# Laying the blank rows of a mixture-of-experts buffer after 12 of 16 token tiles, 640 rows for each expert

## The chip, the core and the metric

The kernel runs on one core of a Trainium2 chip. A core has five engines with instruction queues of their own: TensorE (PE, matrix products; its weight loads are listed apart as PEld), VectorE (DVE), ScalarE (ACT), GpSimd (POOL) and SyncE (SP), which here only issues transfers. Transfers run on 16 DMA engines. Engines wait for one another, and for transfers, through semaphores. Times are device microseconds for the whole program. The profiler's record of one execution gives its span, what each engine did when, and what it waited for.

## The reference

The input `x` has 8 sequences of 256 tokens with 128 numbers each, 2048 tokens in all. Two layers follow, each with a cross-attention to `ctx_1024` and a mixture of experts:

```
x = x + attention0(layernorm(x), ctx)     # 16 heads of 8, a hash mask
x = x + experts0(layernorm(x))            # 8 experts, 512 hidden, relu, biases
x = x + attention1(layernorm(x), ctx)     # 16 heads of 64, causal
x = x + experts1(layernorm(x))            # 8 experts, 352 hidden, silu gate
```

In both expert parts a linear router gives each token 8 logits. The two largest pick its two experts, and their softmax gives the two weights. The layer's output is the weighted sum of the two experts' outputs. So each layer has 4096 (token, expert) pairs.

## The kernel before

**The buffers.** The tokens are 16 tiles of 128 (`NT`). For every layer there is a DRAM tensor `xs` that holds one row of 130 numbers for each pair: the normalised token, the row of `ys` to which its result belongs, and its weight. Each expert has a region of 2176 rows (`XT`) in it, filled from the start. Experts work on tiles of 128 rows, and the last tile of each region is filled only in part. The rest of that tile must hold rows that do no harm: zeros, with a spare row of `ys` as the place of the result. These are the blank rows. A template of 128 of them per expert lies in the DRAM tensor `blank`.

**Routing.** `route` (line 552) handles two or four token tiles: layer norm with both copies of each row written to an SBUF tile `rows` (line 394), the logits, the two maxima, ranks from a matrix product with a triangle, and the running counts `taken`, which hold the number of rows of each expert before every tile. GpSimd then scatters the rows to `xs` (line 644, one indirect DMA for each tile and choice). `norm_T` leaves `lead` steps between the variance and the normalised rows, since GpSimd computes the power in between (line 383).

**Placing.** `place(l, True)` (line 651) runs once 12 tiles (`NEARLY`) are routed. It makes a table of expert tiles that are already full; 16 in layer 0 and 17 in layer 1 (`EARLY`) are worked on from this early table. `place(l, False)` makes the table of the rest (of 39) once all 16 tiles are routed. `tails(l)` (line 696) follows it: it turns the final counts into integers (`last`, line 699), and for each expert loads the count into a register and copies its 128 blank rows behind the last used row (line 706). Four of these copies are issued by SP and four by ACT.

**Experts.** For each expert tile, SP loads its expert and row from the table (line 719), fetches the rows (`xj`, line 733) and the expert's first weights (`wj`, line 740); TensorE flips `xj` (line 745), makes the hidden layer (line 760 in layer 0, 770 and 773 in layer 1) and the result (line 793); VectorE weighs it (line 798), and GpSimd scatters it to `ys` (line 800). Fetches run four tiles ahead of use. `fetch` of the first late tile first lets the side steps run until `tails` has been written down.

**Order.** Every engine runs its instructions in the order in which the program writes them; that order is made by hand. Main loops write the large steps, and `side` is a list of generators of which `tick` runs one step each. `one_by_one` chains generators so that one starts when the one before has ended. In attention 1 a unit (four heads' worth of scores on 256 queries) writes its score products (line 902), four minima on VectorE (`least`, line 917), exponentials on ACT (line 928), and in later units the normalisation on GpSimd (line 941), the flips (line 951) and the values (line 966). Two `tick`s stand in each unit.

**Dependencies.** Waits between transfers that touch the same DRAM tensor follow from the order of writing, unless the kernel declares them disjoint. `free` declares a write disjoint from the others of its key, `after` makes a read wait for the listed writes. A row at an offset held in a register counts as touching the whole tensor.

Of the kernel before, what the change touches and what calls it, by code (L numbers as in the profile page):

```python
# [17 lines left out]
P = 128  # L18
B = 8
S = 256  # L20
QT = S // P
# [11 lines left out]
NT = T // P  # L33
NJ = (2 * T + E * (P - 1)) // P
ROW = D + 2
XT = T + P
NX = E * XT + E * P
# [4 lines left out]
NEARLY = NT - 4  # L42
EARLY = (16, 17)
# [19 lines left out]
def kernel(  # L63
# [28 lines left out]
    nc = tc.nc  # L92
# [20 lines left out]
    known = {}  # L113
# [11 lines left out]
            )  # L125
        return dma

    def free(key, dma, by_index=True):

        tc.declare_no_dep(dma.ins, group=key, reason="disjoint rows")  # L130
        tc.add_to_no_dep_group(key, dma.ins)
        if by_index:
            tc.declare_no_dep(dma.ins, group=key + "read", reason="disjoint rows")
            if key in known:
                tc.add_to_no_dep_group(key + "late", dma.ins)
        writes.setdefault(key, []).append(dma)


    side = []

    def tick():
        for g in list(side):
            if next(g, side) is side:
                side.remove(g)
# [8 lines left out]
    def one_by_one(g):  # L153


        def run():
            while turn:
                yield from turn[0]
                turn.pop(0)

        turn.append(g)
        if len(turn) == 1:
            side.append(run())

    def drain():
        while side:
# [9 lines left out]
    xt = [xb[i // QT][:, i % QT, :] for i in range(NT)]  # L176
# [194 lines left out]
    def norm_T(tiles, name, rows=None, lead=2):  # L371
        n = len(tiles)
        mv = sm.tile([P, GT, 2], F32, tag="mv", name=f"mv{name}", bufs=3)
        for i, t in enumerate(tiles):
            st = sm.tile([P, 6], F32, tag="bn", name=f"st{name}_{i}", bufs=3)
            nc.vector.bn_stats(out=st, in_=t)
            nc.vector.bn_aggr(out=mv[:, i, :], in_=st)
            if i == 1 and n > 2:
                yield
        ve = sm.tile([P, GT], F32, tag="ve", name=f"ve{name}", bufs=3)  # L380
        nc.vector.tensor_scalar(ve[:, :n], mv[:, :n, 1], EPS, None, ALU.add)
        rs = sm.tile([P, GT], F32, tag="rs", name=f"rs{name}", bufs=3)
        nc.gpsimd.tensor_tensor(rs[:, :n], ve[:, :n], mhalf[:, :n], ALU.pow)
        for _ in range(lead):
            yield
        xns = []
        for i, t in enumerate(tiles):
            if rows is None:
                xn = sm.tile([P, D], F32, tag="xn", name=f"xn{name}_{i}", bufs=4)
                to = xn  # L390
            else:
                xn = rows[:, i, 0, :D]
                to, t = rows[:, i, :, :D], t.unsqueeze(1).to_broadcast([P, 2, D])
            nc.vector.tensor_scalar(to, t, mv[:, i, 0:1], rs[:, i : i + 1], ALU.subtract, ALU.mult)
            xns.append(xn)
            if i == 1 and n > 2:
                yield
        for _ in range(1 if rows is None else 2):
            yield
        pt = bank("pt", f"np{name}")  # L400
        for i, xn in enumerate(xns):
            nc.tensor.transpose(pt[:, ts(i, P)], xn, ident)
        tag, bufs = (f"xnT{n}", 2) if rows is None else (f"xnTr{n}" if n == QT else f"xnT{n}", 1)
        xnT = wk.tile([P, n * P], F32, tag=tag, name=f"xnT{name}", bufs=bufs)
        nc.scalar.copy(xnT, pt[:, : n * P])
        yield
        return xnT
# [144 lines left out]
    def route(l, t0, GT, eng=nc.vector):  # L552

        name = f"{l}_{t0}"
# [1 line left out]
        tiles = slice(t0, t0 + GT)  # L556
        rows = wk.tile([P, G // P, 2, ROW], F32, tag="rows", name=f"rows{name}")[:, :GT]
        nc.gpsimd.tensor_copy(rows[:, :, :, D].bitcast(I32), dest[:, tiles, :])
        xnT = yield from norm_T(xt[tiles], f"r{name}", rows)
        pl = bank("pt", f"pl{name}")  # L560
        for i in range(GT):
            nc.tensor.matmul(pl[:, ts(i, E)], lhsT=xnT[:, ts(i, P)], rhs=wr, start=True, stop=True)
# [133 lines left out]
    def tails(l):  # L696

        last = sm.tile([P, E], I32, tag="last", name=f"last{l}", bufs=1)
        nc.vector.tensor_copy(last, taken[l][:, NT, :])
        for i in range(E):  # L700
            if i % 2 == 0:
                yield
                yield
            eng = (nc.sync, nc.scalar)[i % 2]
            row = eng.value_load(last[0:1, i : i + 1], min_val=0, max_val=NX - P)
            free(f"xs{l}", eng.dma_start(out=xs[l][bass.ds(row, P), :], in_=blank[ts(i, P), :]), False)
        tabs[l, "blank"] = True

    def experts(l):
        ch = (CH0, CH1)[l]  # L710
# [14 lines left out]
            regs[j] = (e, row, pe)  # L725

        def fetch(j):
            while j >= EARLY[l] and (l, "blank") not in tabs:
                tick()
            e, row, _ = regs[j]  # L730
            xj = wk.tile([P, ROW], F32, tag="xj", name=f"xj{l}_{j}", bufs=10)
            after(
                nc.sync.dma_start(out=xj, in_=xs[l][bass.ds(row, P), :]), f"xs{l}",
                known[f"xs{l}"] if j < EARLY[l] else None,
            )
            src = (wa0, wa1)[l]
            if j % 2 == 0:
                tiles["w"] = wk.tile([P, 2, 2 * FF1], F32, tag="pr", name=f"wj{l}_{j}", bufs=3)
            wj = tiles["w"][:, j % 2, : src.shape[2]]
            nc.sync.dma_start(out=wj, in_=src[bass.ds(e, 1), :, :].rearrange("o p w -> p (o w)"))  # L740
            tiles[j] = {"x": xj, "w": wj}
# [242 lines left out]
    def attention1(begin):  # L984
        n = B * NU
        when = ((3, 3, 3, 3), (1, 1, 2, 3), (0, 1, 2, 3))
        for k in range(n + 4):
            b, w = divmod(k, NU)
            here, flips = k < n, 0 <= k - 2 < n
            if here:  # L990
                scores1(k)
                if w == 0 and 1 <= b and b + 2 < B:
                    side.append(enter1(b + 2))
            if 0 <= k - 1 < n:
                normalise(k - 1)
            bo, wo = divmod(k - 6, NU)
            if 0 <= bo < B and wo in (0, 1):
                output(bo, wo)
                if wo == 1 and bo + 1 < B:
                    one_by_one(route(1, QT * bo, QT))  # L1000
                    if QT * (bo + 1) == NEARLY:
                        one_by_one(place(1, True))
            nxt = b + 1 < B and here
            for z in range(3):
                if flips:
                    flip1(k - 2, z)
                if here:
                    least(k, z)
                if nxt and z < 2:
                    project(b + 1, w, "kv"[z])  # L1010
                elif nxt:

                    for i in range(NU):
                        if when[min(b, 2)][i] != w:
                            continue
                        project(b + 1, i, "q")
                if here:
                    exps(k, z)
            tick()
            if here:  # L1020
                least(k, 3)
            if flips:
                values1(k - 2)
            if here:
                exps(k, 3)
            tick()
            if k < 3 or k >= n - QT:
                tick()
            if k >= n + 1:
                begin(range(2 * (k - n - 1), 2 * (k - n)) if k < n + 3 else ())  # L1030
# [35 lines left out]
    for n in range(NS * B + LAG + 3):  # L1066
        b, i = divmod(n, NS)
        if n < NS * B:
            scores(b, i)
        if 0 <= n - LAG < H * B:  # L1070
            probs(*divmod(n - LAG, H))
        g, r = divmod(n - LAG - 5, 4)
        if r == 0 and 0 <= g < 4 * B:
            values0(*divmod(g, 4))
            if g % 2:
                side.append(finish0(g // 4, g % 4 // 2))
        if i in (HH, 0) and HH <= n <= NS * B:
            side.append(maxima((n - 1) // NS, 1 if i == 0 else 0))
        if i == 2 and b + 2 < B:
            side.append(prep0(b + 2))  # L1080
        if i == 6 and b in (3, 5, 7):
            one_by_one(route(0, 2 * (b - 3), GT, nc.gpsimd))
            if b == 7:
                one_by_one(place(0, True))
                one_by_one(route(0, NT - 2 * QT, QT))
        if n == NS * B + 8:
            side.append(keys_values(0))
        tick()
        if n == NS * B + LAG - 2:
            begin0(range(4))  # L1090
            tiles0 = run0()
        if n >= NS * B + LAG:
            next(tiles0)
    one_by_one(route(0, NT - QT, QT))
    one_by_one(place(0, False))
    one_by_one(tails(0))
    first = None
    for j in tiles0:
        if j == FIRST + 2:
# [18 lines left out]
    for j in run1():  # L1118
        if j == 0:
            one_by_one(route(1, NT - QT, QT))  # L1120
            one_by_one(place(1, False))
            one_by_one(tails(1))
    drain()
    for b in range(B):
        side.append(combine(1, b))
# [64 lines left out]
```

## Time and profile before

| | us |
|---|---|
| median of 3 runs | 775.32 (767.14 to 777.8) |
| the profiled execution | 743.06 |
| its span, first to last instruction | 741.3 |

| engine | busy us | share of the span |
|---|---|---|
| PE | 628.3 | 85% |
| PEld (beside PE) | 484.7 | 65% |
| DVE | 478.9 | 65% |
| ACT | 333.3 | 45% |
| POOL | 326.3 | 44% |

The profiled execution was 4% shorter than the median of the runs. Its mean granted TensorE clock was 0.950 of full speed. By TensorE's record, layer 0's attention ends near 229 us, where the first expert tile is flipped; layer 1's first flip is at 628.76 us. From 345 to 612 us the core is in attention 1. At the end, from about 722 us, results are read back and added.

An entry of the waits gives engine, line, what was waited for, then total us, times and the longest. An entry in order of time gives start, duration, engine, line, operation and tiles, how many were merged, and in brackets the idle time before it with what ended it.

### The profile page before, as it was taken

Reading aid. Unit: us, or ns where it says so; the run is one execution under the profiler, and the core shown is the slowest. Engines: PE = TensorE matmul, PEld = TensorE weight load, DVE = VectorE, ACT = ScalarE, POOL = GpSimd, SP = SyncE. Lnnn points to the kernel's source line nnn. Section 1 sums busy time; section 2 is a strip of 40 time slices with the busy share of each in tenths; the row PEclk is TensorE's granted clock in tenths of the full one; section 3 lists DMA queues with packets and bytes.
Section 4 is the critical chain, followed back from the end, with each engine's and each line's share of the span. In section 5 each row is a group of like instructions: output and inputs, shape, how many; then the busy total and the mean of one; then the engine's idle time right before and its main releaser. Section 6 shows DMA issues by size and latency. Waiting matters only on the chain. (4 is left out here: it accounts for less than half of the span.)

```text
span 741.3 us, 15222 instructions
## 1 busy us (share of the span) xinstructions
PE 628.3 (85%) x4781; PEld 484.7 (65%) x4781; DVE 478.9 (65%) x1804; ACT 333.3 (45%) x1028; POOL 326.3 (44%) x393
## 2 busy tenths in 40 slices
PE   2179887888898789988999999999999888898990
PEld 1145454444546779985777777777768566898990
DVE  4287787677846544555677788778786865643442
ACT  1015555446542122335656656556565662433330
POOL 4144537626062354435343353535353542563442
PEclk9999999788969899999999999999999998999995
DMA  3667876845005557724011300000000004658846
GB/s 89 68 160 229 227 195 181 197 129 159 2 30 142 135 140 203 203 86 114 15 57 37 93 16 15 15 16 16 1 16 1 16 16 142 173 161 232 247 143 177
DMA packets 71799, 79.60 MB, mean 107 GB/s; under 512 B 9712, under 2 KB 55688, under 8 KB 70712
## 3 DMA queue, kind: packets, MB, share of 16 engines
q1 hardware_dynamic: 62624, 59.00, 30.0%
q0 software_dynamic: 7600, 18.64, 8.5%
q10 hardware_dynamic: 1496, 0.99, 0.9%
q8 instruction: 39, 0.64, 0.4%
q14 instruction: 40, 0.33, 0.1%
HBM read 56.60 MB, written 26.34 MB: 112 GB/s over the span
## 5 line engine op out<-in xcount | busy, mean ns | idle before, releaser
L928 ACT ACTIVATE p<-ns,nm 128x256 f32<-128x256 f32 (+1 forms) x256 | 113.9, 448 | 48.2 <-DVE nm L917 47.4
L941 POOL TENSOR_TENSOR p<-p,rd 128x1024 f32<-128x1024 f32 (+1 forms) x63 | 92.2, 1482 | 68.6 <-DVE rd L936 68.5
L800 POOL DMA_INDIRECT ys<-yj,xj x78 | 75.6, 969 | 87.0 <-DVE yj L798 59.6
L484 DVE TENSOR_REDUCE mx<-sc 128x2 f32<-128x512 f32 x128 | 83.9, 684 | 27.6 <-PE sc L480 27.2
L518 ACT ACTIVATE pT<-st 128x512 f32<-128x512 f32 x128 | 73.9, 595 | 59.0 <-PE st L511 58.4
L644 POOL DMA_INDIRECT xs<-rows,ati x64 | 63.2, 988 | 72.0 <-DVE rows L636 44.7
L917 DVE CUSTOM_DVE_ANT_0 ns<-s,tri 128x256 f32<-128x256 f32 (+1 forms) x256 | 78.8, 350 | 0.5 <-PE s L902 0.5
L480 PE MATMUL sc<-k,q 74*128 74x256 bf16 x256 | 56.5, 310 | 16.0 <-DVE mx L484 9.0
L902 PE MATMUL s<-k,q 64*128 64x256 f32 (+1 forms) x512 | 61.8, 343 | 7.0 <-DVE nm L917 7.0
L953 ACT COPY pT<-pt 128x512 f32<-128x512 f32 x64 | 36.8, 575 | 66.9 <-PE pt L951 66.9
L511 PE MATMUL st<-q,k 77*128 77x256 bf16 x256 | 55.9, 306 | 11.9 <-DMA q<-mT 6.7
L951 PEld LDWEIGHTS pt<-ident,p 128*128 128x128 f32 x384 | 47.3, 146 | 21.1 <-DVE k L868 8.1
L902 PEld LDWEIGHTS s<-k,q 64*128 64x128 f32 x512 | 47.4, 186 | 20.8 <-DVE nm L917 11.8
L951 PE MATMUL pt<-ident,p 128*128 128x128 f32 x384 | 59.0, 283 | 2.2 <-POOL p L941 2.2
L966 PE MATMUL o<-pT,v 128*64 128x256 f32 (+1 forms) x512 | 54.6, 340 | 3.9 <-ACT pT L953 3.7
L763 ACT ACTIVATE h<-ph,wj 128x128 f32<-128x128 f32 x78 | 24.4, 364 | 60.8 <-issue 37.6
L480 PEld LDWEIGHTS <-q 74*128 74x128 bf16 x256 | 24.7, 108 | 39.4 <-issue 34.2
L779 DVE TENSOR_TENSOR h<-s,pu 128x256 f32<-128x256 f32 x78 | 24.0, 349 | 40.1 <-PE px L745 32.2
L966 PEld LDWEIGHTS o<-pT,v 128*64 128x64 f32 x512 | 34.7, 139 | 22.9 <-issue 7.1
L760 PE MATMUL ph<-xT,wj 128*128 128x128 f32 x312 | 46.2, 293 | 3.0 <-DVE xT L747 3.0
L928 ACT ACTIVATION_READ_ACCUMULATOR p<-ns,nm 128x1 f32 x256 | 48.4, 189 | 0.0
L793 PE MATMUL y<-w,h 128*128 x312 | 45.6, 291 | 0.0
(218 smaller groups left out, 1269.9 us busy)
## 6 DMA issues: line engine op xcount, KB each, us to landing
wj<-wa SPq DMA_DIRECT2D x39, 352.0 KB
wj<-wa SPq DMA_DIRECT2D x39, 258.0 KB
rows<-part SPq DMA_DIRECT2D x42, 192.0 KB
xj<-xs SPq DMA_DIRECT2D x78, 65.0 KB
yy<-ys SPq DMA_DIRECT2D x16, 256.0 KB
q<-rows SPq DMA_DIRECT2D x7, 576.0 KB
k<-rows SPq DMA_DIRECT2D x7, 576.0 KB
wa<-in_w POOLq DMA_DIRECT2D x8, 256.0 KB
```

What stands on the lines that cost most here:

```text
L480: nc.tensor.matmul(sc[:, k, :], lhsT=q9s[b % 3][:R_MAX, h, ts(qt, P)], rhs=k9s[b % 3][:R_MAX, h, :], start=True, stop=True,)
L484: pace[0] = nc.vector.tensor_reduce(c0[b]["mx"][:, qt, 2 * u : 2 * u + 2], sc, AX.X, ALU.max)
L511: nc.tensor.matmul(st[:, ts(t, S)], lhsT=k9s[b % 3][:R_ALL, h, ts(t, P)], rhs=q9s[b % 3][:R_ALL, h, :], start=True, stop=True,)
L518: nc.scalar.activation(pT.rearrange("p t s -> p (t s)"), st, AF.Exp)
L644: nc.gpsimd.indirect_dma_start(out=xs[l][:, :], out_offset=to, in_=rows[:, i, k, :], in_offset=None),
L800: free(f"ys{l}", nc.gpsimd.indirect_dma_start(out=ys[l][:, :], out_offset=to, in_=yj, in_offset=None))
L902: nc.tensor.matmul(u["s"][a, r][:, (1 - qt) * S : (1 - qt) * S + n], lhsT=c1[b]["q"][rows, c, ts(qt, P)], rhs=c1[b]["k"][rows, c, :n], sta ...
L917: nc.vector.tensor_tensor_reduce(out=ns[:, o : o + n], in0=s[:, o : o + n], in1=tri[:, S - n :], scale=-1.0, scalar=3.0e38, op0=ALU.add, o ...
L928: nc.scalar.activation(p[:, o : o + n], ns[:, o : o + n], AF.Exp, bias=nm[:, a : a + 1], scale=-1.0, accum_out=u["sum"][:, 2 * i + a : 2 * ...
L941: eng.tensor_tensor(p, p, rd[:, :, a : a + 1].to_broadcast([P, 4, n]), ALU.mult)
L951: nc.tensor.transpose(pt[:, ts(n, P)], u["p"][:, i, (S, 0, P)[m] :][:, :P], ident)
L966: nc.tensor.matmul(o[DK1 * r : DK1 * (r + 1), a, t * P :], lhsT=v[:, t, cols], rhs=pT, start=(t == 0), stop=True, skip_group_check=True,)
```

## The change

There are four edits.

- `tails(l)` is no longer a link of the chain behind `place(l, False)`. A new helper `beside` puts it among the side steps as soon as `place(l, True)` has ended, in both layers, so it reads the counts after 12 tiles. As the remaining four tiles may add up to 512 rows to an expert, it writes 5 x 128 = 640 rows for each, from the count after 12 tiles on. One copy for each expert reads the same 128-row template five times. All eight copies are issued by SP.
- These copies do not go through `free` any more, and `fetch` no longer holds the late tiles until `tails` is done. `free` loses its parameter `by_index`.
- `route` gives `norm_T` a lead of 4 steps for the last two tiles and 2 for others.
- In attention 1 the first `tick` of a unit stands behind `least(k, 3)`, the fourth minimum, instead of ahead of it.

```diff
-    def free(key, dma, by_index=True):
+    def free(key, dma):
...
+    def beside(g):
+        side.append(g)
+        return
+        yield
...
-        xnT = yield from norm_T(xt[tiles], f"r{name}", rows)
+        xnT = yield from norm_T(xt[tiles], f"r{name}", rows, lead=4 if t0 == NT - QT else 2)
...
     def tails(l):
 
         last = sm.tile([P, E], I32, tag="last", name=f"last{l}", bufs=1)
-        nc.vector.tensor_copy(last, taken[l][:, NT, :])
+        nc.vector.tensor_copy(last, taken[l][:, NEARLY, :])
+        m = NT - NEARLY + 1
         for i in range(E):
             if i % 2 == 0:
                 yield
-                yield
-            eng = (nc.sync, nc.scalar)[i % 2]
-            row = eng.value_load(last[0:1, i : i + 1], min_val=0, max_val=NX - P)
-            free(f"xs{l}", eng.dma_start(out=xs[l][bass.ds(row, P), :], in_=blank[ts(i, P), :]), False)
-        tabs[l, "blank"] = True
+            row = nc.sync.value_load(last[0:1, i : i + 1], min_val=0, max_val=NX - m * P)
+            to = xs[l][bass.ds(row, m * P), :].rearrange("(c p) w -> c (p w)", p=P)
+            src = blank[ts(i, P), :].rearrange("(o p) w -> o (p w)", o=1)
+            nc.sync.dma_start(out=to, in_=src.to_broadcast([m, P * ROW]))
...
         def fetch(j):
-            while j >= EARLY[l] and (l, "blank") not in tabs:
-                tick()
...
                         one_by_one(place(1, True))
+                        one_by_one(beside(tails(1)))
...
-            tick()
             if here:
                 least(k, 3)
+            tick()
...
                 one_by_one(place(0, True))
+                one_by_one(beside(tails(0)))
...
     one_by_one(place(0, False))
-    one_by_one(tails(0))
...
             one_by_one(place(1, False))
-            one_by_one(tails(1))
```

More of the change, by code (lines that the diff above doesn't have):

```diff
@@ L126, in after @@
         return dma
-    def free(key, dma, by_index=True):
+    def free(key, dma):
         tc.declare_no_dep(dma.ins, group=key, reason="disjoint rows")
         tc.add_to_no_dep_group(key, dma.ins)
[L132 to L135, printed above, removed]
+        tc.declare_no_dep(dma.ins, group=key + "read", reason="disjoint rows")
+        if key in known:
+            tc.add_to_no_dep_group(key + "late", dma.ins)
         writes.setdefault(key, []).append(dma)
```

## The prediction, made before the changed kernel was run

> **What bounds the kernel now.** I read the page's busy rows first, then the waits of SP's DMA queue, then SP and TensorE in order of time round the places where the blank rows are written and read.
>
> ```profile
> PE 628.3 (85%) x4781; PEld 484.7 (65%) x4781; DVE 478.9 (65%) x1804; ACT 333.3 (45%) x1028; POOL 326.3 (44%) x393
> ```
>
> TensorE is busy for most of the span, and in both expert stages (about 231 to 345 us and 629 to 722 us) one tile follows the other every 2.1 us. So a stage ends when TensorE's list ends, and a gap in that list is paid in full. SP's queue feeds it. Its longest wait, then its issues in order of time (start, length, line, tiles):
>
> ```profile
> SPq L719 <- DVE tab L686: 131.5, 2, 125.5
> ...
> 221.52 0.40 SPq L733 DMA_DIRECT2D xj<-xs  x1
> ...
> 268.94 3.94 SPq L706 DMA_DIRECT2D xs<-blank  x3
> 274.78 0.36 SPq L733 DMA_DIRECT2D xj<-xs  x1
> ...
> 617.99 0.36 SPq L733 DMA_DIRECT2D xj<-xs  x1
> ```
>
> SP idles before each first fetch (L733 at 221.52 and 617.99): it waits for the early table and the scatters of tiles 0 to 11, so there is no slack in front of these fetches on SP. The slack lies behind them, on TensorE:
>
> ```profile
> 229.09 0.33 PE L745 MATMUL px<-ident,xj 128*128 128x128 f32 x1
> 231.29 1.16 PE L760 MATMUL ph<-xT,wj 128*128 128x128 f32 x8 [1.87 <-DVE xT L747]
> ...
> 240.19 1.16 PE L760 MATMUL ph<-xT,wj 128*128 128x128 f32 x8
> ...
> 247.08 0.80 PE L402 MATMUL npr<-ident,rows 128*128 128x128 f32 x2 [3.51 <-DVE rows L394]
> ...
> 267.39 1.16 PE L760 MATMUL ph<-xT,wj 128*128 128x128 f32 x8 [1.15 <-DVE xT L747]
> ...
> 276.80 0.33 PE L745 MATMUL px<-ident,xj 128*128 128x128 f32 x1 [1.90 <-DMA xj<-xs]
> ...
> 629.41 0.93 PE L770 MATMUL ph<-xT,wj 128*128 128x128 f32 x6 [0.36 <-ACT xT L747]
> ...
> 633.68 0.83 PE L770 MATMUL ph<-xT,wj 128*128 128x128 f32 x6
> ```
>
> Expert tile 0 starts at 231.29 and 629.41, behind what is left of attention; tile 4 of layer 0 at 240.19, tile 2 of layer 1 at 633.68. The brackets are what today's order costs: 3.51 us (tile 14's route waits for GpSimd), and 1.15 and 1.90 us round the late blanks.
>
> **What the change removes.** The late blanks go from the path: 1.15 + 1.90 us in layer 0; in layer 1 the four TensorE gaps on xj and wj between 663 and 679 us (0.29, 0.87, 1.19, 0.99), where SP mixes value loads and blanks with fetches: 3.3 us. The larger lead on tile 14 takes the 3.51 us. In all 6.6 us in layer 0 and 3.3 us in layer 1. The routing of the last tiles stays as it is; tile 16's fetch has four tiles (8 us) of lead over it.
>
> **What it adds: a chain.** In the changed program's instruction order on SP, six of the eight blanks stand ahead of the first xj fetch in both layers, and the other two between fetches (layer 0: behind the fourth, layer 1: behind the second). They are no longer declared disjoint, so blank 1 waits for the last scatter of tiles 0 to 11, each blank for the one before it to land, xj_0 for blank 6, blank 7 for the fetches already out, the next xj for blank 8. On GpSimd the scatters of tiles 12 and 13 wait for blank 8, with expert results queued behind them. SP has nothing else to do meanwhile; every fetch stands behind the chain.
>
> The price of one link. Before, the third SP blank of 268.94 was issued at about 272.35 and xj_16, which waited for it, at 274.78: 2.4 us for 65 KB. It had 16 rows of 4160 bytes, one to an engine. The new copy moves 333 KB in the order 5x2x8320 (outer size 5, step 0 in the source). No row shows such a copy, so I bound it. By the rows alone, a copy loads all 16 engines: 333 KB / 16 = 20.8 KB each. The trace's packet records for 4160 bytes are 159 ns at best and 195 ns median, that is 26 and 21 bytes per ns, so 1.0 us less the 0.2 that is in the 2.4: a link of 3.15 us. The Trainium skill says otherwise ("DMA: Bandwidth & Descriptors", Rules for kernel authors, use all 16 engines): an outermost dimension of c < 16, its example being a zero-step broadcast, holds the whole copy to at most c engines. Then each of five engines carries 66.6 KB, 2.5 us at 26 bytes per ns, 3.0 at 22. The upper bound comes from the 8192-byte packets (492 ns median, 16.7 bytes per ns) and, at 15, is 4.5 us; a gain is excluded, since more bytes go over no more engines. Link: 4.8 to 6.7 us. I take 5.2, from the 4160-byte copies, which like this one stay in DRAM. By the row's 16 engines the whole sum below comes to +26 us, by the rule to +58; I go with the rule, because the shape on SP is just the one it describes.
>
> **Layer 0.** `last` stands behind the k copy of 220.60 on VectorE and is done near 221.6; before, its end at 262.88 and the first blank at 264.18 lie 1.3 us apart, so blank 1 goes at 222.8. Six links: 222.8 + 31.2 = 254.0 for xj_0, 32.5 us late. wj_0 is issued 0.7 us later; its 258 KB take 0.95 us at 272 GB/s (204 GB/s at a DMA share of 0.75 between 280 and 320 us) plus 2.2 fixed: 257.9 for tile 0 against 231.29. That is +26.6, so TensorE's leftover attention hid 5.9. The fourth xj lands near 260; two more links give 270.4, xj_4 270.5, wj_4 landed 274.4, tile 4 there against 240.19: +34.2. Less 6.6: **+27.6 us.** Tile 14's rows wait for GpSimd behind the scatters held to 270.4 (4 x 1.27 us, landing, power: near 278.3) and stand behind tile 5's hidden layer (277.8): under 1 us, counted as nothing.
>
> **Layer 1.** `last` stands behind the statistics of tile 12 (620.4), blank 1 at 622.1, xj_0 at 653.3 (before 617.99), wj_0 landed 657.4 (352 KB): tile 0 at +28.0. xj_1 lands near 656.7; blanks 7 and 8, behind wj_1 on the rings, to 667.5; wj_2 landed 671.7, tile 2 there against 633.68: +38.0. Less 3.3: **+34.7 us.** GpSimd's four held scatters end near 673, and tile 0's result follows; its buffer is asked for by tile 3's result near 677: nothing.
>
> **The side steps in attention 1.** Behind the fourth minimum, their VectorE work no longer holds the score banks. What that can give is the idle time in this answer (345 to 612 us, engine, line, releaser, total):
>
> ```profile
> PE s L902 <- DVE nm L917: 6.8, 9, 2.9
> ```
>
> Weight loads wait 10.6 us for the same, mostly at the same moments: 0 to 8 us to win. The steps themselves come 0.6 us later in a unit (the minimum's instructions, 533.48 to 534.1 us), and their readers are half a unit or more away, so a loss is at most 2. I take **-4 us**. ACT loses its eight value loads and blanks, the cause of the 1.15 above.
>
> **Sum.** 27.6 + 34.7 - 4 = +58.3 us. The profiled execution took 743.06 us (span 741.3 and 1.8 around it) and would take 801. The runs' median is 775.32, 4% above it; the chain is DMA latency and is added whole: 833.6.
>
> **Rivals.**
> 1. *The copy spreads over 16 engines, still chained* (3.15 us a link): xj_0 at 241.7 and 641.0, tile 4 at 258.0 (+17.8), tile 2 at 655.3 (+21.6), less 9.9 and 4: +26, 801 us. For it: every blank so far did spread. Against: the shape. Chance 0.12.
> 2. *Large pieces run slow* (33 KB each, all five engines reading one source): 6.7 us a link, +39.7 and +46.7, less 4: +82, 858 us; beyond that if they fight over the source. For it: the 8192-byte packets; against: those end in SBUF. Chance 0.14.
> 3. *Not slower.* The blanks overlap and hide under attention's rest: SP issues one in 1.3 us (3.94 for three), six in 7.8, and cover is 5.9 in layer 0 and 7.3 in layer 1, so tile 0 loses some 3 us each time and 9.9 + 4 come back: -8, 767 us. It decides from a link of about 1.5 us downward. Against it: 2.4 us for a fifth of the bytes, and the waits in the program. Chance 0.05.
> 4. *The late waits stay.* The blanks move, but tile 16's fetch still waits, now for the scatters of tiles 14 and 15, which the held GpSimd queue pushes back. Then the 3.05 and 3.3 us aren't won back: +65, 840 us. Against it: those scatters go out near tile 8 of layer 0 and tile 6 of layer 1, eight and more tiles ahead. It lies inside the main range and in its chance.
>
> **How the numbers follow.** Main case 0.69: 833.6, own range 827 to 858 (links 4.8 to 6.7). With rivals 1 and 2 the range is 798 to 864. Two per cent, 15.5 us, is about what a measurement of this kernel can tell from no change: slower 0.94, within 0.05, faster 0.01.
>
> **What would show it.** SP: six line-711 copies some 5 us apart from 223 and 622 us, the first xj at about 254 and 653, then two more copies before the fifth and third xj. TensorE: idle from about 229 to 256 and 629 to 655, then gaps near 8 us (from 266) and 10 us (from 662). Packets over 8 KB. GpSimd's first scatter of tile 12 held until blank 8. In attention 1, L902's row shrinks (now L904). It is wrong if links are far from 5.2 us, or if the xj are issued ahead of the blanks' landing.

## The result, and the profile after

The changed kernel took 820.55 us (median of four runs, 818.01 to 827.09) against 775.33 for the kernel before: a ratio of 1.062, with a 95% interval of 1.0535 to 1.0705. The ratio is the one on record; that of the two medians is 1.058. That is slower, by 45 us where 58 were forecast. The profiled execution of the changed kernel took 820.45 us, with a span of 818.7.

First the busy row of the page of the changed kernel.

```profile
PE 633.9 (77%) x4781; PEld 486.7 (59%) x4781; DVE 474.6 (58%) x1804; ACT 332.3 (41%) x1028; POOL 325.8 (40%) x393
```

Every engine has about as much work as before, and all shares fell. The time was added as waiting. Next are the waits of SP's queue in the changed kernel (line, what was waited for, then total us, times and the longest). Its lines have moved: 711 is now the blank copy, 735 the fetch of rows, 747 the flip of these rows on TensorE.

```profile
SPq L708 <- DVE last L703: 141.2, 2, 125.9
SPq L711 <- DMA xs<-blank: 36.2, 12, 3.4
SPq L735 <- DMA xs<-blank: 8.6, 4, 3.3
```

Line 711 waits twelve times for another blank copy, and a fetch waits four times for one: that is twice for each layer, as the forecast placed it. The same queue in order of time, cut to blanks and first fetches (start, length, line, tiles, how many merged):

```profile
236.51 27.66 SPq L711 DMA_DIRECT2D xs<-blank  x6
268.67 0.40 SPq L735 DMA_DIRECT2D xj<-xs  x1
...
275.01 5.75 SPq L711 DMA_DIRECT2D xs<-blank  x2
285.36 0.36 SPq L735 DMA_DIRECT2D xj<-xs  x1
...
659.12 25.41 SPq L711 DMA_DIRECT2D xs<-blank  x6
688.64 0.38 SPq L735 DMA_DIRECT2D xj<-xs  x1
...
693.12 5.95 SPq L711 DMA_DIRECT2D xs<-blank  x2
703.38 0.36 SPq L735 DMA_DIRECT2D xj<-xs  x1
```

Six blanks, a fetch behind them, then two blanks and the fetch of tile 4 (layer 0) or tile 2 (layer 1). From the first blank to the first fetch it is 268.67 - 236.51 = 32.2 us in layer 0 and 29.5 in layer 1, so a link took 5.4 and 4.9 us. TensorE's answer in order of time, with the idle time before each in brackets:

```profile
270.58 0.45 PE L747 MATMUL px<-ident,xj 128*128 128x128 f32 x1 [25.39 <-DMA xj<-xs]
272.17 2.05 PE L762 MATMUL ph<-xT,wj 128*128 128x128 f32 x8 [1.14 <-DMA wj<-wa]
...
287.29 0.44 PE L747 MATMUL px<-ident,xj 128*128 128x128 f32 x1 [5.21 <-DMA xj<-xs]
...
690.61 0.45 PE L747 MATMUL px<-ident,xj 128*128 128x128 f32 x1 [24.09 <-DMA xj<-xs]
692.90 1.62 PE L772 MATMUL ph<-xT,wj 128*128 128x128 f32 x6 [1.84 <-DMA wj<-wa]
...
705.21 0.47 PE L747 MATMUL px<-ident,xj 128*128 128x128 f32 x1 [7.25 <-DMA xj<-xs]
707.37 1.62 PE L772 MATMUL ph<-xT,wj 128*128 128x128 f32 x6 [0.22 <-DMA wj<-wa]
```

These are the four holes. The flips waited 25.39 + 5.21 + 24.09 + 7.25 = 61.9 us for rows, and with the weights behind them (1.1 us in layer 0, 2.1 in layer 1) TensorE waited 65.1 us for expert inputs. In the first profile of before, it was 6.5.

### The profile page after: what moved, and what is told of

The parts are those of the page before. It is cut to its first block, busy times and chain, and to the rows that moved or that the text cites. A ratio compares the mean times of both kernels' runs of the same rounds, so it can differ in the third digit from the quotient of the medians.

```text
span 818.7 us, 15232 instructions
## 1 busy us (share of the span) xinstructions
PE 633.9 (77%) x4781; PEld 486.7 (59%) x4781; DVE 474.6 (58%) x1804; ACT 332.3 (41%) x1028; POOL 325.8 (40%) x393
## 5 line engine op out<-in xcount | busy, mean ns | idle before, releaser
L919 DVE CUSTOM_DVE_ANT_0 ns<-s,tri 128x256 f32<-128x256 f32 (+1 forms) x256 | 76.9, 348 | 0.5 <-PE s L904 0.5
L747 PE MATMUL px<-ident,xj 128*128 128x128 f32 x78 | 22.5, 288 | 61.9 <-DMA xj<-xs 61.9
L904 PE MATMUL s<-k,q 64*128 64x256 f32 (+1 forms) x512 | 53.2, 338 | 0.5 <-DVE nm L919 0.5
L747 PEld LDWEIGHTS px<-ident,xj 128*128 128x128 f32 x78 | 11.6, 148 | 63.2 <-issue 55.7
L904 PEld LDWEIGHTS s<-k,q 64*128 64x128 f32 x512 | 42.8, 186 | 10.3 <-issue 4.5
```

The lines of the kernel that those rows point to most:

```text
L904: nc.tensor.matmul(u["s"][a, r][:, (1 - qt) * S : (1 - qt) * S + n], lhsT=c1[b]["q"][rows, c, ts(qt, P)], rhs=c1[b]["k"][rows, c, :n], sta ...
L919: nc.vector.tensor_tensor_reduce(out=ns[:, o : o + n], in0=s[:, o : o + n], in1=tri[:, S - n :], scale=-1.0, scalar=3.0e38, op0=ALU.add, o ...
```

## The experiments

Each kernel was timed beside the kernel before on the same chip. A ratio is this kernel's time over that of before, with its 95% interval. The last column is what TensorE waited for `xj` and `wj` in the profiled execution (a4's is not compared, since that execution was 8 us above the median of its runs).

| kernel | us | before | ratio | waits us |
|---|---|---|---|---|
| changed | 820.55 | 775.33 | 1.062 (1.0535 to 1.0705) | 65.1 |
| a1, before again | 779.56 | 777.23 | 1.0051 (1.0013 to 1.0088) | 5.6 |
| a2, copies over 16 engines | 797.84 | 777.23 | 1.0271 (1.0208 to 1.0334) | 36.5 |
| a3, copies not chained | 793.84 | 777.23 | 1.0238 (1.0153 to 1.0322) | 40.3 |
| a4, side steps alone | 763.34 | 777.23 | 0.9802 (0.974 to 0.9864) | |
| b1, lead alone | 779.78 | 776.13 | 1.0024 (0.9986 to 1.0062) | 7.1 |
| b3, blanks free, on ACT | 769.6 | 776.13 | 0.9895 (0.9845 to 0.9945) | 0 |
| b4, side steps and lead | 766.85 | 776.13 | 0.9892 (0.9861 to 0.9923) | 5.8 |
| b5, changed without side steps | 841.6 | 776.13 | 1.0838 (1.0798 to 1.0877) | 68.6 |
| c2, a2 and a3 together | 751.54 | 748.63 | 1.0039 (1.0003 to 1.0076) | 19.7 |
| c3, side steps alone again | 738.08 | 748.63 | 0.9858 (0.9829 to 0.9888) | 6.4 |

### Is the profile of before typical? (a1)

The kernel before was run once more, with no edit.

> The kernel before, profiled once more. The profiled execution that the prediction was read from took 743 us, the runs around it 775, so 32 us of ordinary time were not in it. Theory A (the clock): an execution of ordinary length shows a lower granted TensorE clock, and its extra time lies in stages in which TensorE is busy throughout (attention 0, experts 0), not in waits for transfers. Then layer 0's first flip comes some 15 us later than at 229 us, as in the changed kernel's profile, and the remaining 15 us or so lie in stages that the chain of blanks relieves by letting TensorE rest. Theory B: the extra time is spread evenly over the span, 4% everywhere, or lies in transfers. Time: 775 us, ratio 1.00.

It differs from itself by 0.5%, with an interval that leaves 1 out. So half a per cent is what such a comparison can be off by. Its profiled execution took 782.77 us, 40 more than the one that the forecast was made from. About half of that, 21 us, lies ahead of layer 0's first flip, which came at 250.29 us and not at 229.09. Below is one window in the first profile of before, then in a1: the window, its length, busy time of PE, PEld, DVE, ACT and POOL with instruction counts, then the granted TensorE clock, the DMA share and GB/s.

```profile
150.00:200.00 50.00, 43.17 (x372) 24.96 (x372) 39.40 (x116) 27.83 (x55) 17.59 (x29) 0.90 0.36 98
150.00:200.00 50.00, 39.12 (x276) 22.30 (x274) 30.11 (x86) 21.36 (x42) 16.61 (x29) 0.73 0.45 119
```

The clock granted in a1 was lower, and TensorE got through fewer instructions. Next is the stretch from the first fetch on SP to the first flip, again in the first profile of before and then in a1:

```profile
221.50:229.10 7.60, 6.56 (x42) 3.62 (x40) 4.43 (x13) 2.06 (x4) 0.88 (x2) 1.00 0.55 146
237.00:250.30 13.30, 11.88 (x52) 6.06 (x49) 6.46 (x18) 3.74 (x7) 0.88 (x2) 0.75 0.41 107
```

This is what TensorE still had to do of attention 0 when the fetch went out: 7.6 us in one, 13.3 in the other. Two things make the difference. In a1 TensorE was ten instructions further from the end at that moment (52 against 42), and the same list ran slower. From the product `pk` below, which stands at the same place in both, it was 229.09 - 219.47 = 9.6 us to the first flip in before and 250.29 - 237.83 = 12.5 in a1:

```profile
219.47 1.10 PE L865 MATMUL pk<-c,wk 128*128 128x256 f32 x4 [0.24 <-DVE on L544]
237.83 2.05 PE L865 MATMUL pk<-c,wk 128*128 128x256 f32 x4 [0.39 <-DVE on L544]
250.29 0.33 PE L745 MATMUL px<-ident,xj 128*128 128x128 f32 x1
```

The cover in front of layer 0's first tile is thus no fixed number of microseconds. The later comparisons by stage are made against a1.

### The width of the copy, and the chain (a2, a3, c2)

a2 splits the copy so that its outermost size is 16; it stays chained.

```diff
-            to = xs[l][bass.ds(row, m * P), :].rearrange("(c p) w -> c (p w)", p=P)
-            src = blank[ts(i, P), :].rearrange("(o p) w -> o (p w)", o=1)
-            nc.sync.dma_start(out=to, in_=src.to_broadcast([m, P * ROW]))
+            to = xs[l][bass.ds(row, m * P), :].rearrange("(c z p) w -> z c (p w)", c=m, z=16)
+            src = blank[ts(i, P), :].rearrange("(z p) w -> z (p w)", z=16)
+            src = src.unsqueeze(1).to_broadcast([16, m, P // 16 * ROW])
+            nc.sync.dma_start(out=to, in_=src)
```

> The changed kernel with each blank copy's dimensions turned so that 16 is the outermost (16x5x1040 for 5x2x8320): same bytes, same chain. Theory A (five engines carry a copy): a link falls from 5.1 to about 3.15 us, by 2 us for each of eight links and two layers, 32 us in all: about 790 us, xj_0 some 12 us earlier behind the first blank. Rival (large pieces are slow, or the latency of a link is all, whatever the engines): links stay within 0.5 us of 5, time within 8 us of 820.

SP of a2 in order of time, layer 0:

```profile
240.86 17.31 SPq L712 DMA_DIRECT2D xs<-blank  x6
261.18 0.40 SPq L736 DMA_DIRECT2D xj<-xs  x1
```

Six links now take 20.3 us, 3.4 each, where the forecast's 16-engine link was 3.15. The kernel is 22.7 us faster than the changed one, by the two medians, where 30 were expected; TensorE's waits fell by 65.1 - 36.5 = 28.6. So the shape of the copy made each link some 2 us longer. In the trace's packet records a copy of the changed kernel is 10 packets of 33,280 bytes, five started at a time; in a2 all are of 4160 bytes, up to 19 at once by their recorded times. The packets of one of layer 0's first copies last 3.3 to 3.5 us from first to last, and 1.5 to 1.7 in a2, which is the difference; some 2 us of each link are beside the packets in both.

a2 changes the size of the pieces along with the width. The large pieces are not slow in themselves: the second five of a copy took 1.23 us each, 27 bytes per ns, where a 4160-byte piece took 159 ns at best, 26 bytes per ns. The first five took about 2 us in layer 0. What slows those is not shown.

a3 keeps the five pieces and declares the eight copies of a layer disjoint from one another.

```diff
-            nc.sync.dma_start(out=to, in_=src.to_broadcast([m, P * ROW]))
+            dma = nc.sync.dma_start(out=to, in_=src.to_broadcast([m, P * ROW]))
+            tc.declare_no_dep(dma.ins, group=f"blank{l}", reason="disjoint rows")
+            tc.add_to_no_dep_group(f"blank{l}", dma.ins)
```

> The changed kernel with the eight blank copies declared disjoint from one another (they are: 640 rows from a count of at most 1536 end inside a region of 2176); they still wait for the scatters, and the fetches for them. Theory A (the chain of landings is the cost): the copies follow at SP's pace or at the five engines' pace, 3 us each, so six take about 18 us and a landing in place of 31: 10 us less before the first fetch in each layer and 2 us less for the last two: about 796 us. If latency alone is the cost, six take 10 us: about 785. Rival (the bytes on five engines are all of it): 6 x 5 us remain, 820 us.

SP of a3, layer 0:

```profile
233.54 11.67 SPq L711 DMA_DIRECT2D xs<-blank  x6
252.91 0.40 SPq L737 DMA_DIRECT2D xj<-xs  x1
```

The six copies go out 2.1 us apart and wait for none, yet the first fetch still stands 19.4 us behind the first of them. Six copies of 333 KB over five engines are 400 KB for each engine. From the first issue to the fetch that is 20.6 bytes per ns, near the 22 to 26 that the forecast took for an engine. In the packet records these pieces run five at a time and back to back, mostly 1.23 us each, from 235.1 us until just before the fetch. So either repair alone leaves a bound of nearly the same size: a2 the latency of six waits, a3 the rate of five engines. What spaces the issues by 2.1 us is not shown.

c2 makes both edits.

> The changed kernel with both repairs at once: 16x5x1040 and disjoint from one another, still ahead of the first fetch. With only the chain broken the copies were issued 2.1 us apart but xj_0 came 19.4 us behind the first, since five engines had to work off 400 KB each; with only the spread, 20.3 us behind. Theory A (each repair left the other cost standing): SP's pace of 2.1 us is now all, xj_0 comes 14 us behind the first copy in both layers, and the time falls 10 to 14 us below either, to 780 to 785 (ratio 1.008). Rival (the two repairs save the same microseconds, so something else holds the first fetch near 19 us): 793, ratio 1.024.

SP of c2, layer 0:

```profile
224.02 7.98 SPq L712 DMA_DIRECT2D xs<-blank  x6
235.71 0.40 SPq L738 DMA_DIRECT2D xj<-xs  x1
```

The first fetch stands 11.7 us behind the first blank (10.9 in layer 1), TensorE's waits fall to 19.7 us, and the kernel is within 0.4% of before. But c2 also has the gain of the side steps, so the fair comparison is c3 on the same chip, which has the same side steps and no early blanks. Against it c2 is 13.5 us slower, 1.8%; the changed kernel, by the two ratios, is 1.062 / 0.9858, or 7.7%, slower. So chain and width together make about three quarters of the loss. TensorE's longer waits for expert inputs are as much as the rest: 19.7 - 6.4 = 13.3 us. In c2 the copies still stand ahead of the first fetch; in b3 below they don't, and TensorE has no such wait.

### The side steps, alone and taken away (a4, c3, b5)

a4 and c3 are the kernel before with this one edit; b5 is the changed kernel without it.

```diff
-            tick()
             if here:
                 least(k, 3)
+            tick()
```

> The kernel before with only the side steps moved behind the fourth minimum. Theory A: attention 1 loses the idle time of TensorE on the score banks; the stretch from the first to the last score product falls from 269 to 262 us, as it did between the two profiles, and the time by about 7 us, to 768 (ratio 0.99). Rival (the 7 us between the profiles are the clock or the later blanks): within 2 us of 775.

> The kernel before with only the side steps moved, once more with more rounds, since its first measurement (ratio 0.980) lies further below 1 than the 10.5 us that its stretch of attention 1 lost. If 10.5 us are all: ratio 0.986 and about 766 us; if something outside attention 1 gains as well: 0.980.

> The changed kernel with the side steps put back ahead of the fourth minimum. If the side steps are worth the same here as in the kernel before (14 us there), 834; if the chain of blanks hides part of it (attention 1 ends earlier, but the chain starts with the scatters and not with TensorE), less than 8 us above 820.

The edit gives 2.0% in a4 and 1.4% in c3, 13.9 and 10.6 us; taken away, it costs 1.0838 against 1.062, 2%. Its ratios are the lowest of all that were run, though the intervals of b3 and b4, which have the same edit, reach into them. In the forecast its gain was 4 us, with 8 as the most. The group of score products in a1, and their weight loads (count, then busy us and mean ns, then idle us before it with its releasers):

```profile
L902 PE MATMUL s<-k,q 64*128 64x256 f32 (+1 forms) x512 | 59.8, 344 | 4.8 <-DVE nm L917 4.8
L902 PEld LDWEIGHTS s<-k,q 64*128 64x128 f32 x512 | 46.8, 188 | 17.2 <-DVE nm L917 7.6 <-issue 4.5 <-DVE k L868 0.8
```

The same groups in the changed kernel:

```profile
L904 PE MATMUL s<-k,q 64*128 64x256 f32 (+1 forms) x512 | 53.2, 338 | 0.5 <-DVE nm L919 0.5
L904 PEld LDWEIGHTS s<-k,q 64*128 64x128 f32 x512 | 42.8, 186 | 10.3 <-issue 4.5 <-DVE nm L919 1.9 <-DVE k L870 0.8
```

And in c3:

```profile
L902 PE MATMUL s<-k,q 64*128 64x256 f32 (+1 forms) x512 | 53.8, 341 | 0.5 <-DVE nm L917 0.5
```

The products' idle column, the one that the forecast went by, falls by 4.3 us. But the busy column falls by another 6.6, for the same 512 products. So part of the wait had been counted as busy time. This is no accident of one profile: the group is busy for 59.1 to 61.8 us in the four profiles with the old order that were read (before, a1, b1, b5), and for 53.2 to 54.1 in the eight with the new one. The weight loads' wait for the minima falls too, by 5.7 us; how far it coincides with the other two is not shown. Idle and busy time of the products fall by 10.9 us together, and that is just by how much the stretch from the first to the last score product is shorter. This stretch in a1, as a window:

```profile
361.60:634.40 272.80, 256.27 (x1873) 195.40 (x1874) 197.89 (x892) 163.27 (x601) 120.06 (x102) 0.99 0.10 29
```

and in the changed kernel:

```profile
381.20:643.10 261.90, 249.02 (x1873) 190.00 (x1874) 200.88 (x893) 162.63 (x601) 120.39 (x102) 1.00 0.11 30
```

The same 1873 PE instructions, at nearly the same clock, are busy for 256.27 us in one and 249.02 in the other. In b5 the stretch is back at 272.3 us.

### The lead (b1, b4)

b1 is the kernel before with the lead of 4 for the last two tiles; b4 has the side steps too.

```diff
-        xnT = yield from norm_T(xt[tiles], f"r{name}", rows)
+        xnT = yield from norm_T(xt[tiles], f"r{name}", rows, lead=4 if t0 == NT - QT else 2)
```

> The kernel before with only the lead of 4 steps for the last two tiles. Theory A (the 3.5 us gap of TensorE at layer 0's tile 14 goes, as read in the first profile): -2 to -3.5 us, ratio 0.996. Theory B (on an execution of ordinary length that gap isn't there, or another takes its place at once): within 1 us, ratio 1.00.

> The kernel before with the side steps moved and the lead of 4. If the parts add: 763 and the lead's 2 to 3.5, 760 to 761; if the lead does nothing, 763. Against the version with free blank copies it tells what laying them early is worth: theory A says some 5 us.

b1's interval holds 1, and b4 is no faster than a4. Where these ran, the lead is worth nothing that can be measured. The profiles show why: the 3.51-us wait that it was to take is not there in a1, which has the old lead. It is there in c3, with the old lead too, and smaller in c2, with the new one. The flip of tile 14's rows in a1, c3 and c2:

```profile
271.10 0.38 PE L402 MATMUL npr<-ident,rows 128*128 128x128 f32 x2
255.92 0.79 PE L402 MATMUL npr<-ident,rows 128*128 128x128 f32 x2 [3.59 <-DVE rows L394]
260.36 0.65 PE L406 MATMUL npr<-ident,rows 128*128 128x128 f32 x2 [1.55 <-DVE rows L398]
```

What the lead is worth on its own in executions like c3's was not measured.

### Is it good to lay the rows early, if that costs nothing? (b3)

b3 is the changed kernel with the wide copies issued by ACT and declared disjoint from one another, from the scatters of tiles 0 to 11 and from the early fetches.

```diff
-            row = nc.sync.value_load(...)
+            row = nc.scalar.value_load(...)
...
-            nc.sync.dma_start(out=to, in_=src.to_broadcast([m, P * ROW]))
+            dma = nc.scalar.dma_start(out=to, in_=src)
+            key = f"xs{l}"
+            for group in (key, key + "read", key + "blank"):
+                tc.declare_no_dep(dma.ins, group=group, reason="disjoint rows")
+            tc.add_to_no_dep_group(key + "blank", dma.ins)
+            tc.add_to_no_dep_group(key + "late", dma.ins)
```

> The changed kernel with the blank copies taken out of the fetches' way: 16x5x1040, issued by ACT, declared disjoint from one another, from the scatters of tiles 0 to 11 and from the early fetches; the scatters of tiles 12 to 15 and the late fetches still wait for them. Theory A (all of the loss is the wait of the first fetches behind the chain; laying the rows early is sound otherwise): the loss of 57 us against the kernel with only the side steps moved (763) vanishes and the late waits are saved, 6 us: 757, between 752 and 765. Rival (the 2.66 MB per layer of extra copying, or GpSimd's held scatters, cost by themselves): stays above 775.

The loss is gone: 0.9895, with b4, which lays the old rows late, at 0.9892. So early rows that hold up no fetch are, as built here, neither better nor worse; the 757 us expected of them were not reached. By TensorE's record layer 0's expert stage (first to last flip) is 2.3 us shorter than in b4, 100.4 against 102.7. But in layer 1 the first flip comes 17.3 us behind the first fetch, and 9.8 in b4. ACT in order of time in b3:

```profile
636.84 10.06 ACTq L712 DMA_DIRECT2D xs<-blank  x4
646.95 0.37 ACT L409 COPY xnTr<-npr 128x256 f32<-128x256 f32 x1 [10.63 <-DMA wj<-wa]
```

Its first four copies take 10 us to issue; the profile puts the wait down to a transfer of weights that SP had issued, and why ACT has to wait for it is not shown. A routing copy stood behind them, and TensorE's logits behind that; its entry in the same order:

```profile
647.37 1.02 PE L566 MATMUL pl<-wr,xnTr 128*128 128x8 f32 x4 [6.31 <-ACT xnTr L409]
```

The gain of 2.3 us in one layer was more than lost to a new wait of 17.3 - 9.8 = 7.5 in the other. A variant that lets the blanks of the changed kernel follow the first fetches wasn't tried: they would then stand behind later scatters, which they must precede.

## Why the prediction was right, and where its size was off

The direction and mechanism hold. The sum, +58.3 us, is set here against the stages of the changed kernel's profiled execution less those of a1's, by TensorE's record. That difference, 37.7 us in spans, is not the 45.2 of the medians, since a1's profiled execution is 3 us above its own median and 7 above the median of before in the result.

| term of the sum | predicted us | measured us |
|---|---|---|
| layer 0, tile 0 | +26.6 | 25.39 + 1.14 = +26.5 |
| layer 0, tile 4, beyond tile 0 | +7.6 | +5.2 |
| layer 1, tile 0 | +28.0 | 24.09 + 1.84 = +25.9 |
| layer 1, tile 2, beyond tile 0 | +10.0 | 7.25 + 0.22 = +7.5 |
| stalls removed, layer 0 | -6.6 | -8.7 |
| stalls removed, layer 1 | -3.3 | -4.2 |
| side steps in attention 1 | -4 | -10.9 |
| end of attention 0 | 0 | -5.1 |
| rest | 0 | +1.5 |
| sum | +58.3 | +37.7 |

The holes are TensorE's idle times above. The stalls removed are the change of each expert stage (first to last flip) without these holes: in layer 0, 103.7 became 101.4 us with 5.21 + 1.14 of holes in it, so -8.7; in layer 1, 100.0 became 105.1 with 1.84 + 7.25 + 0.22, so -4.2. These two rows are remainders and hold whatever else differs between two executions: the kernel before alone took 98.4 and 103.7 us for the first stage in its two profiles, and 89.4 and 100.0 for the second. That the stalls went is seen in the waits; how much they were worth is not. The end of attention 0 came at 245.19 us in one execution and 250.29 in the other.

- **The chain.** Right in place, order and count. The link was forecast at 5.2 us with the Trainium skill's rule ("DMA: Bandwidth & Descriptors", Rules for kernel authors) that an outermost size of five holds a copy to five engines; six links gave 5.4 and 4.9. a2, with the same bytes, had links of 3.4. The four holes were to be 72.2 us and are 65.1, within a tenth.
- **"The chain is DMA latency and is added whole" to the median.** This held: chain less stalls removed was to be +62.3. b5, which is the chain with the lead and without the side steps, is 1.0838, which is 65 us on 776.13.
- **The side steps: this step failed in size.** "What that can give is the idle time in this answer" took the products' idle column for nearly all of the wait, set the weight loads' 10.6 us aside as the same moments, and put 8 us as the most. The runs show 10.6 and 13.9 us, and 10.9 in the stretch itself, 6.6 of it inside the busy column. Of the 13 us between forecast and medians this term is 7 to 10.
- **The lead.** Its credit of 3.51 us came from a wait that a1 does not have, and b1 shows no gain. The stalls that did go in layer 0 were others, among them a wait of 3.9 us for rows behind the late blanks in a1. The first profile did not have it in that size: there the wait was 1.9.
- **The second pair of links.** Both were to cost more than they did, 17.6 us against 12.7. In layer 0 the first four tiles after the hole were slower than the 2.1 us each that was counted (flips at 270.58 and, for tile 3, 9.2 us later), which left more cover. In layer 1 links were shorter, 4.9 us in the mean.
- **Cover in front of layer 0.** The forecast counted 5.9 us. Here attention 0 ended 8.7 us behind the first blank, and so hid more, but six links took 32.2 us and not 31.2, and the hole came out as forecast. That is partly luck, since a1 shows that the cover depends on the clock and on how far TensorE has come.
- **The rivals.** Copies over 16 engines, and copies slower than 5.2 us, fall by the links. "Not slower" falls with them; even with chain and width both gone, c2 is 0.4% slower than before and not 8 us faster: six copies were issued in 8.0 us, close to the 7.8 counted, but the fetch waits until they have landed and came 11.7 us behind the first. That the late waits stay was not seen.
- **GpSimd.** The scatters held until blank 8 were costed at nothing, and TensorE's waits in the expert stages name neither GpSimd nor a scatter. Two of its idle times there, 2.6 and 3.6 us, have no releaser in the profile, so a small cost is not excluded.
- **Restart.** That TensorE's products run slower for some microseconds behind each hole was not in the sum. By the estimate in the last section this is 7 to 8 us for the four holes, hidden in the two rows of stalls removed.

## What to carry to other kernels

Before a write is moved ahead of a read, count what the dependency tracker will put between them: writes at register offsets to one tensor are a chain, and each link pays a whole transfer's latency (5.4 and 4.9 us here), so declare what is disjoint and give a copy an outermost size that reaches all engines. That took about three quarters of the loss away here; the rest went only when the copies no longer stood ahead of the fetch. Where an engine waits inside a group of products, compare the group's busy time with that of a kernel without the wait: the products' idle column alone understated a gain here by more than half. Before slack is read from one profile, see how far its time lies from the median, since a cover of 7.6 us in one execution was 13.3 in another.

## What was not expected of the hardware

- **Restart after a long idle.** In the changed kernel's first hole PE did nothing and the granted clock was 0.50. It stayed at 0.50 for nearly 6 us after the flip at 270.58 that ended the hole, and as long behind the hole in layer 1, whose flip is at 690.61:

```profile
250.00:270.00 20.00, 0.00 (x0) 0.00 (x0) 0.00 (x0) 0.00 (x0) 0.00 (x0) 0.50 0.19 61
270.60:276.40 5.80, 4.66 (x29) 3.04 (x29) 2.19 (x12) 0.62 (x2) 0.00 (x0) 0.50 0.67 211
276.60:286.60 10.00, 5.48 (x48) 5.23 (x47) 3.58 (x13) 2.27 (x7) 2.97 (x3) 1.00 0.21 70
690.70:696.20 5.50, 3.47 (x14) 2.80 (x14) 0.29 (x1) 2.24 (x5) 0.00 (x0) 0.50 0.57 170
```

  The first six hidden-layer products of layer 1 then took 1.62 us, as the entry at 692.90 shows, and the next tile's six took 0.93. Adding up such differences for all products in that stretch (0.69 and 0.66 for two groups of six, 0.18 and 0.15 for two flips) gives an estimate of 1.7 us; by the same count the other three holes give 1.4 to 2.3 each. So a long wait costs more than its length, by about 2 us each time.
- **The shape of a copy sets its issue time too.** In the answer for the blanks' line (min, median and max ns of an issue), the 5 x 2 x 8320 copies of the changed kernel:

```profile
L711 SPq DMA_DIRECT2D xs<-blank x16: 785/800/871, 236.5 to 698.3; - x16
```

  and the copies of a2, 80 pieces instead of 10 with the same bytes:

```profile
L712 SPq DMA_DIRECT2D xs<-blank x16: 557/572/703, 240.9 to 678.1; - x16
```

  The medians repeat: 807 in a3 and 799 in b5, with the first shape, and 574 in c2 with the second. What in the shape makes the difference is not shown.

- **The same work at another level.** In the batch with c2 and c3 the kernel before took 748.6 us, and 775 to 777 in the others. That batch ran on another chip; whether the chip makes the level is not shown. The first profile of before, at 743.06, is like it: its expert stages took 98.4 and 89.4 us, in c3 97.3 and 89.2, in a1 103.7 and 100.0. For the one edit that was timed at both levels, the side steps, the ratios are 0.9802 and 0.9858, half a per cent apart.
